# A selective scan on one core: the tiles that feed it, cut in half

## The chip, the cores and the metric

The kernel runs on one core of a Trainium2 chip. The core has four engines that compute: TensorE (PE, with its weight loads PEld), VectorE (DVE), ScalarE (ACT) and GpSimd (POOL). SyncE (SP) issues nearly all of this kernel's DMA transfers, one after the other in the order of its queue. The metric is device time in microseconds (us) of one execution.

## The reference, cut to what matters

Two layers on an image batch x of shape (4, 384, 32, 32). The first is a selective scan in four directions (rows, columns, and both backwards) with a normalization and GELU, followed by a mixture of four experts of which each token takes two. The second is attention and a small feed-forward layer. The change touches the scan alone:

```python
xs = _cross_scan(x)                               # 4 directions k, 1024 positions l
x_dbl = jnp.einsum('bkdl,kcd->bkcl', xs, x_proj_weight)
dts, Bs, Cs = (x_dbl[:, :, :R], x_dbl[:, :, R:R + N], x_dbl[:, :, R + N:])   # R = 12, N = 16
dts = jnp.einsum('bkrl,kdr->bkdl', dts, dt_projs_weight)
A = -jnp.exp(A_logs.astype(jnp.float32)).reshape(K, D, N)
dt = jax.nn.softplus(dts + dt_projs_bias[None, :, :, None])
...
def step(h, inp):
    dtt, ut, bt, ct = inp
    dA = jnp.exp(dtt[..., None] * A)
    h = h * dA + (dtt * ut)[..., None] * bt[:, :, None, :]
    y = jnp.einsum('bkdn,bkn->bkd', h, ct)
    return (h, y)
```

For each of 384 channels d and 16 states n there is one recurrence along the 1024 positions. It needs dt and dt * u of its channel, and B and C of its state.

## The kernel before, in words

**Stages.** `scan_layer` goes through 32 units: 4 images b, 4 directions k, 2 halves of 512 positions (`HF = 512`). After the last unit of an image, `finish` normalizes it, and `between` starts the tail of the image before: its experts (`experts`, eleven slots of 256 tokens), its attention and its last layers. A scheduler orders the instructions of each engine by its own timeline, so that the tail of image b - 1 stands between the instructions of the scan of image b. Only the tail of the last image comes after the scan. Each engine, SP too, works through its instructions in the order so fixed.

**Projection.** `project` (L287) makes a unit's inputs, one unit ahead. A matmul gives dt, B and C for 512 positions (`xd_ps`, L312), ACT copies it (`xd`), SP stores the B and C rows in DRAM (`rows`, L318), and loads them back into `bcs` tiles, each row spread over 32 partitions (L325). Then, in three parts of 128 channels, ACT, POOL (L360, L361) and DVE (L366, L367) make dt and dt * u, and SP stores both in DRAM (`dd`, L369 and L370).

**A tile's layout.** The 128 partitions of a scan instruction hold 32 channels times 4 states. So `bcs` has B and C of 4 states in 4 bands of 32 partitions, and the 16 states make 4 groups (`NG = 4`). `dtr` has 32 channels repeated for the 4 states, for two blocks of channels side by side (j = 0, 1). One `bcs` tile holds B and C (t) of two groups, 8 KB per partition; one `dtr` tile holds dt (s = 0) and dt * u (s = 1) of two blocks, 8 KB per partition. Both come from pools with three buffers. Each band and each t or s is a transfer of its own, 128 KB: 8 for a tile.

**The scan.** `chunk` (L373) does 128 channels of a unit; a unit has three chunks, the whole scan 96. It loads two `dtr` tiles (q = 0, 1; L386). Then, for each of the 4 groups and each q:
- POOL multiplies dt * u by B for both blocks (L401, 1024 elements per partition),
- ACT makes exp(dt * A) into `da` in PSUM, one instruction per block (L410); `da` has two buffers,
- DVE scans (L415), one instruction per block,
- for q = 1, DVE multiplies by C (L422); for q = 0, POOL does (L429),
- PE sums over the states into `acc` (L436), one instruction per block.

POOL thus has three instructions of 1024 elements per group, twelve per chunk. In its queue, L401 of a group usually stands some instructions ahead of L429 of the group before.

**When a buffer is free.** A `dtr` tile is last read in the fourth group of its chunk, by POOL's L401 (dt * u) and by ACT's second L410 (dt). A `bcs` tile is last read in the third chunk of its unit, by POOL's L429 and DVE's L422. The load of the next tile in that slot waits for these on SP's queue, and everything behind it on that queue waits with it: other `dtr` and `bcs` loads, the stores of `dd` and `rows`, and in the expert stage the weights (`w<-in_w`, 576 KB each, L757 and L765), which wait for PE to be done with their slot.

Of the kernel before, what the change touches and what calls it, by code (L numbers as in the profile page):

```python
# [9 lines left out]
F32 = mybir.dt.float32  # L10
I32 = mybir.dt.int32
AF = mybir.ActivationFunctionType
# [5 lines left out]
P = 128  # L18
# [5 lines left out]
HF = 512  # L24
# [20 lines left out]
DB = 32  # L45
NB = D // DB
NJ = P // DB
NG = NS // NJ
# [56 lines left out]
def halves(i):  # L105
    return slice(i * HF, (i + 1) * HF)


class Body:
# [76 lines left out]
    def scan_layer(self, x1, between):  # L186

        nc, tc, a = self.nc, self.tc, self.a
        with ExitStack() as ctx:
# [58 lines left out]
            for n, unit in enumerate(units):  # L248
# [3 lines left out]
                if n + 1 < len(units):  # L252
                    nb = units[n + 1][0]
                    if nb not in us:
                        us[nb] = start(nb)
                    project = self.project(units[n + 1], us[nb], wx, work, dram, psum, ahead)
                    next(project)
# [29 lines left out]
    def project(self, unit, u, wx, work, dram, psum, made):  # L287

        nc, a = self.nc, self.a
        b, k, i = unit
        by_cols = k % 2 == 1
        w = slice(i * (HW // NH), (i + 1) * (HW // NH))

        def part(c):
            if by_cols:
                return u[:, c, :].rearrange("p (h w) -> p w h", h=HW)[:, w, :]
            return u[:, c, halves(i)]  # L300

        def split(ap):
            return ap.rearrange("p (w h) -> p w h", h=HW) if by_cols else ap

        def k2(name, shape=(P, HF)):
            return work.tile([*shape], F32, tag="k2", name=name, bufs=6)

        wdt = k2("wdt", (R, D))
        nc.sync.dma_start(out=wdt, in_=a["wdt"][:, k, :])
        ps = psum.tile([P, HF], F32, tag="ps", name="xd_ps")  # L310
        for c in range(DC):
            nc.tensor.matmul(  # L312
                split(ps[:XD, :]), wx[:, c, k, :], part(c), start=(c == 0), stop=(c == DC - 1)
            )
        xd = k2("xd", (XD, HF))
        nc.scalar.copy(xd, ps[:XD, :])
        rows = dram.tile([2 * NS, HF], F32, tag="rows", name="rows")
        nc.sync.dma_start(out=rows, in_=xd[R:XD, :])  # L318
        view = rows.rearrange("(t g n) l -> n t g l", t=2, g=NG)
        bcs = []  # L320
        for h in range(NG // 2):
            bc = work.tile([P, 2, 2, HF], F32, tag="bcs", name="bcs", bufs=3)
            for n in range(NJ):
                for t in range(2):
                    nc.sync.dma_start(  # L325
                        out=bc[n * DB : (n + 1) * DB, t],
                        in_=view[n, t, 2 * h : 2 * h + 2].partition_broadcast(DB),
                    )
            bcs.append(bc)

        dd = dram.tile([2, D, HF], F32, tag="dd", name="dd")
        made += [bcs, dd]
        yield

        def begin(c):
            ps = psum.tile([P, HF], F32, tag="ps", name="dt_ps")
            nc.tensor.matmul(ps, wdt[:, c * P : (c + 1) * P], xd[:R, :], start=True, stop=True)  # L340
            bias = self.col("dtb", k * DC + c)
            mag, one_e, lnw = k2("mag"), k2("one_e"), k2("lnw")
            nc.scalar.activation(mag, ps, AF.Abs, bias=bias)
            nc.scalar.activation(ps, ps, AF.Relu, bias=bias)
            nc.scalar.activation(mag, mag, AF.Exp, scale=-1.0)
            nc.scalar.activation(one_e, mag, AF.Identity, bias=1.0)
            nc.scalar.activation(lnw, one_e, AF.Ln)
            nc.scalar.activation(one_e, one_e, AF.Identity, bias=self.minus1)  # L348
            return ps, mag, one_e, lnw

        def behind(engine):
            if self.place_behind is None:
                return nullcontext()
            return self.tc.issue_after(self.place_behind[engine])

        for c in range(DC):
            ps, mag, one_e, lnw = begin(c)
            yield
            with behind("pool"):
                nc.gpsimd.tensor_sub(mag, one_e, mag)  # L360
                nc.gpsimd.tensor_sub(lnw, lnw, mag)  # L361
            yield
            d, du = mag, one_e
            rows = slice(c * P, (c + 1) * P)
            with behind("dve"):
                nc.vector.tensor_add(ps, ps, lnw)  # L366
                nc.vector.tensor_mul(split(du), split(ps), part(c))  # L367
            nc.scalar.copy(d, ps)  # L368
            nc.sync.dma_start(out=dd[0, rows, :], in_=d)  # L369
            ins = nc.sync.dma_start(out=dd[1, rows, :], in_=du).ins  # L370
        made.append(ins)

    def chunk(self, unit, first, c, fed, carry, nega, sel, acc, work, dap):  # L373

        nc = self.nc
        b, k, i = unit
        bcs, dd, _ = fed
        dtr = []  # L380
        for q in range(NJ // 2):
            t = work.tile([P, 2, 2, HF], F32, tag="dtr", name="dtr", bufs=3)
            at = c * P + q * 2 * DB
            for n in range(NJ):
                for s in range(2):
                    nc.sync.dma_start(  # L386
                        out=t[n * DB : (n + 1) * DB, s],
                        in_=dd[s, at : at + 2 * DB, :].rearrange("(j d) l -> d j l", d=DB),
                    )
            dtr.append(t)  # L390

        def run(ap):
            return ap[:, ::-1] if k >= 2 else ap

        last = 0 if k >= 2 else HF - 1
        for g in range(NG):
            bc = bcs[g // 2]
            out = []
            for q in range(NJ // 2):
                bx = work.tile([P, 2, HF], F32, tag="bx", name="bx", bufs=6)  # L400
                pool = nc.gpsimd.tensor_mul(  # L401
                    bx, dtr[q][:, 1], bc[:, 0, g % 2].unsqueeze(1).to_broadcast([P, 2, HF])
                ).ins
                cg = bc[:, 1, g % 2]
                at = ((c * 2 + q) * NG + g) * 2
                for j in range(2):
                    block = c * NJ + 2 * q + j
                    col = (k * NB + block) * NG + g
                    da = dap.tile([P, HF], F32, tag="da", name="da")
                    nc.scalar.activation(  # L410
                        da, dtr[q][:, 0, j, :], AF.Exp, scale=nega[:, col : col + 1]
                    )
                    hold = carry[:, at + j : at + j + 1]
                    h = bx[:, j, :] if q == 0 else da
                    nc.vector.tensor_tensor_scan(  # L415
                        run(h), run(da), run(bx[:, j, :]), 0.0 if first else hold,
                        ALU.mult, ALU.add,
                    )
                    if q == 1:
                        if first:  # L420
                            nc.vector.tensor_copy(hold, h[:, last : last + 1])
                        dve = nc.vector.tensor_mul(bx[:, j, :], h, cg).ins  # L422
                if q == 0:
                    if first:
                        for j in range(2):
                            nc.vector.tensor_copy(
                                carry[:, at + j : at + j + 1], bx[:, j, last : last + 1]
                            )
                    pool = nc.gpsimd.tensor_mul(  # L429
                        bx, bx, cg.unsqueeze(1).to_broadcast([P, 2, HF])  # L430
                    ).ins
                out.append(bx)
            for q in range(NJ // 2):
                for j in range(2):
                    lo = (2 * q + j) * DB
                    nc.tensor.matmul(  # L436
                        acc[lo : lo + DB, :], sel, out[q][:, j, :],
                        start=(g == 0), stop=(g == NG - 1),
                    )
            self.place_behind = {"pool": pool, "dve": dve}  # L440
            yield
# [428 lines left out]
    def attention(self, xc, sums, room):  # L870
# [71 lines left out]

        steps = [(t, i, j) for t in range(HEADS // 2) for i in range(NH) for j in range(MB)]
        made = [project(0)]
        ahead = scores(0, made[0][0], 0, 0)
        atts = []
# [363 lines left out]
```

## Time and profile before

| | us |
|---|---|
| Median of 3 runs | 4761.76 (4757.81 to 4772.4) |
| The profiled execution, its own time | 4754.72 |
| its span, first to last instruction | 4751.4 |
| Scan, first to last L401 | 64.1 to 3644.8 |
| POOL busy in the span | 3098.0 |
| of it L401, 768 instructions of 2.376 us | 1802.4 |
| of it L429, 384 instructions of 2.376 us | 911.4 |
| DVE busy | 3005.0 |
| PE busy | 3543.9 |
| ACT busy | 2568.9 |

The median is of runs without the profiler's one execution; the profile explains the latter, so its stages add up to its span of 4751.4 us. "Busy" counts time in which an engine executes. A line such as `X L1 <- Y L2: 10.0, 3, 5.0` among the waits says that X sat idle for 10.0 us in total before its instruction of line 1, in 3 waits, the longest 5.0, each ended by Y's instruction of line 2 or, where it says DMA, by the landing of that transfer. On a time line a bracket shows the idle time just before an instruction and what ended it; runs of like instructions are merged (x11). The costs of SP's transfers stand as the time of their issue, not of their landing.

Where the scan's main engines stood in forty slices of the span (119 us each), tenths busy:

```profile
DVE  4888887778888776977786668896886210001101
...
POOL 5999997688898777778887679978886110001000
```

### The profile page before, as it was taken

The page shows a single profiled execution, that of the slowest core. Times are in us where ns is not written, and L with a number is a line of the kernel's source. Part 1 is how long each engine was busy: PE and PEld are TensorE (multiplying, and loading weights), DVE is VectorE, ACT ScalarE, POOL GpSimd, SP SyncE. Part 2 cuts the span into 40 slices and gives each one's busy share as a digit, 9 for nine tenths or more (in the row PEclk, how much of TensorE's full clock was granted, in tenths as well). Part 3 has the DMA queues.
Part 4 walks back from the last instruction along what each step waited for, and adds up shares of the span by engine and source line. Part 5 has one row for each costly group of instructions (what it writes and reads, how often), then busy time and mean ns, then how long its engine had stood idle before and what let it go on. Part 6 is the DMA issues. An engine that isn't in the chain of part 4 may idle for free.

```text
span 4751.4 us, 46823 instructions
## 1 busy us (share of the span) xinstructions
PE 3543.9 (75%) x13984; PEld 1707.0 (36%) x13984; DVE 3005.0 (63%) x4308; ACT 2568.9 (54%) x4406; POOL 3098.0 (65%) x1515
## 2 busy tenths in 40 slices
PE   4343334579997688757998767866999889998797
PEld 1000001235554222214555422233556655554323
DVE  4888887778888776977786668896886210001101
ACT  4445544446665666555565566756665344333454
POOL 5999997688898777778887679978886110001000
PEclk6555556579998788868999878977999999998797
DMA  4454463468877434446888444446795743342100
GB/s 108 107 125 106 108 165 85 125 206 222 233 213 210 127 93 113 122 137 181 223 225 240 130 138 106 112 123 181 209 253 169 252 159 127 105 132 77 43 16 14
DMA packets 412229, 691.86 MB, mean 146 GB/s; under 512 B 51136, under 2 KB 214336, under 8 KB 411968
## 3 DMA queue, kind: packets, MB, share of 16 engines
q1 hardware_dynamic: 403232, 663.24, 50.6%
q0 software_dynamic: 8192, 25.17, 1.6%
q8 instruction: 112, 1.84, 0.2%
q14 instruction: 149, 1.22, 0.1%
q10 hardware_dynamic: 544, 0.40, 0.0%
HBM read 563.83 MB, written 124.78 MB: 145 GB/s over the span
## 4 chain that ended last, share of the span: by engine, by line
PE 39%; DVE 20%; DMA 11%; POOL 10%; ACT 9%; issue 7%; SPq 3%; another core or an unknown queue 1%; DVEq 0%; POOLq 0%; ACTq 0%
PE h_ps L803 10%; PE y_ps L819 10%; DVE da L415 6%; POOL bx L401 6%; DMA dtr<-dd 6%; DVE bx L415 5%; PE s_ps L911 4%; PE o_acc L960 3%; PE acc L436 3%; POOL bx L429 2%; ACT da L410 2%; DVE bx L422 2%; PE xd_ps L312 2%; DMA bcs<-rows 2%; DMA w<-in_w 2%
## 5 line engine op out<-in xcount | busy, mean ns | idle before, releaser
L401 POOL TENSOR_TENSOR bx<-dtr,bcs 128x1024 f32<-128x1024 f32 x768 | 1802.4, 2376 | 298.4 <-DMA dtr<-dd 167.9
L410 ACT ACTIVATE da<-dtr,nega 128x512 f32<-128x512 f32 x1536 | 1043.7, 689 | 1107.3 <-DVE bx L422 662.4
L429 POOL TENSOR_TENSOR bx<-bx,bcs 128x1024 f32<-128x1024 f32 x384 | 911.4, 2376 | 128.1 <-DVE bx L415 48.4
L436 PE MATMUL acc<-bx,sel 128*32 128x512 f32 x3072 | 543.8, 751 | 536.7 <-POOL bx L429 401.7
L803 PE MATMUL h_ps<-xc,w 128*128 128x256 f32 x3168 | 780.1, 399 | 83.6 <-DVE xc L787 39.0
L819 PE MATMUL y_ps<-w,hs 128*128 128x384 f32 x2112 | 736.7, 501 | 27.0 <-ACT hs L812 21.4
L803 PEld LDWEIGHTS h_ps<-xc,w 128*128 128x128 f32 x3168 | 617.3, 199 | 302.7 <-issue 122.8
L415 DVE TENSOR_TENSOR_SCAN bx<-da,carry,bx 128x512 f32<-128x512 f32 x384 | 473.3, 1269 | 120.5 <-ACT da L410 61.8
L415 DVE TENSOR_TENSOR_SCAN bx<-da,bx 128x512 f32<-128x512 f32 x384 | 453.3, 1210 | 134.3 <-POOL bx L401 82.7
L415 DVE TENSOR_TENSOR_SCAN da<-da,carry,bx 128x512 f32<-128x512 f32 x384 | 477.1, 1274 | 93.3 <-POOL bx L401 56.8
L819 PEld LDWEIGHTS y_ps<-w,hs 128*128 128x128 f32 x2112 | 401.0, 194 | 359.1 <-issue 83.5
L415 DVE TENSOR_TENSOR_SCAN da<-da,bx 128x512 f32<-128x512 f32 x384 | 455.4, 1218 | 101.9 <-POOL bx L401 56.7
L422 DVE TENSOR_TENSOR bx<-da,bcs 128x512 f32<-128x512 f32 x768 | 508.9, 679 | 3.1
L1001 POOL TENSOR_TENSOR xt<-xt,wb 128x3072 f32<-128x3072 f32 x4 | 26.8, 6706 | 688.0 <-DMA wb<-in_wb 688.0
L916 ACT ACTIVATE ex<-s_ps 128x512 f32<-128x512 f32 x512 | 299.7, 591 | 251.8 <-PE s_ps L911 251.2
L436 PEld LDWEIGHTS acc<-bx,sel 128*32 128x32 f32 x3072 | 74.6, 119 | 875.5 <-POOL bx L429 556.6
L911 PE MATMUL s_ps<-w 64*128 64x512 f32 x1024 | 308.4, 679 | 89.0 <-ACT ex L916 88.6
L960 PE MATMUL o_acc<-ex,vt 128*64 128x512 f32 x1024 | 299.9, 664 | 0.7 <-ACT att L968 0.6
L808 ACT ACTIVATE hs<-h_ps,bb 128x256 f32<-128x256 f32 x528 | 211.5, 472 | 159.3 <-PE h_ps L803 152.2
L823 DVE TENSOR_TENSOR y<-y_ps,bb 128x384 f32<-128x384 f32 x88 | 48.3, 549 | 361.0 <-PE y_ps L819 345.5
L360 POOL TENSOR_TENSOR mag<-one_e,mag 128x512 f32<-128x512 f32 x96 | 123.2, 1283 | 96.8 <-ACT one_e L348 96.6
L340 PE MATMUL dt_ps<-xd,wdt 12*128 12x512 f32 x192 | 138.8, 811 | 60.6 <-ACT mag L368 34.9
(189 smaller groups left out, 3777.4 us busy)
## 6 DMA issues: line engine op xcount, KB each, us to landing
w<-in_w SPq DMA_DIRECT2D x352, 576.0 KB
dtr<-dd SPq DMA_DIRECT2D x1536, 128.0 KB
bcs<-rows SPq DMA_DIRECT2D x512, 128.0 KB
dd<-one_e SPq DMA_DIRECT2D x96, 256.0 KB
dd<-mag SPq DMA_DIRECT2D x96, 256.0 KB
rows<-zero SPq DMA_DIRECT2D x88, 192.0 KB
xs<-rows SPq DMA_DIRECT2D x44, 384.0 KB
made<-y SPq DMA_DIRECT2D x44, 384.0 KB
```

What stands on the lines that cost most here:

```text
L401: pool = nc.gpsimd.tensor_mul(bx, dtr[q][:, 1], bc[:, 0, g % 2].unsqueeze(1).to_broadcast([P, 2, HF])).ins
L410: nc.scalar.activation(da, dtr[q][:, 0, j, :], AF.Exp, scale=nega[:, col : col + 1])
L415: nc.vector.tensor_tensor_scan(run(h), run(da), run(bx[:, j, :]), 0.0 if first else hold, ALU.mult, ALU.add,)
L422: dve = nc.vector.tensor_mul(bx[:, j, :], h, cg).ins
L429: pool = nc.gpsimd.tensor_mul(bx, bx, cg.unsqueeze(1).to_broadcast([P, 2, HF])).ins
L436: nc.tensor.matmul(acc[lo : lo + DB, :], sel, out[q][:, j, :], start=(g == 0), stop=(g == NG - 1),)
L803: nc.tensor.matmul(ps[:, r, :], w1[(f + r) // wf][:, c, (f + r) % wf * P : ((f + r) % wf + 1) * P], xc[:, c, :], start=(c == 0), stop=(c = ...
L808: nc.scalar.activation(hs[:, f + r, :], ps[:, r, :], AF.Identity, bias=bb[:, f + r : f + r + 1])
L819: nc.tensor.matmul(out[:, :D], hs[:, f, t * P : (t + 1) * P], w2[f // wf][:, f % wf, :], start=(f == 0), stop=(f == FC - 1),)
L911: nc.tensor.matmul(ps[:, o, :], w[rows, j * P : (j + 1) * P], w[rows, halves(i)], start=True, stop=True,)
L916: ins = nc.scalar.activation(ex[:, o, :], ps[:, o, :], AF.Exp, scale=HD**-0.5, accum_out=sums[:, t, 2 * j + o, i : i + 1],).ins
L960: ins = nc.tensor.matmul(out[cols, :], made[t][1][:, j, cols], ex[:, o, :], start=(j == 0), stop=(j == MB - 1),).ins
```

## The change

The two kinds of input tile are cut in half. A `dtr` tile holds dt or dt * u, not both, and there are seven of 4 KB for three of 8 KB (28 KB for 24 KB per partition). A `bcs` tile holds B and C of one group, not of two, and there are five of 4 KB for three of 8 KB (20 KB for 24 KB). The transfers stay as many, and each moves 128 KB as before; those of `bcs` take B and C of one group in place of B or C of two. The order in which the loads are written changes with it: for `dtr`, all four bands of dt come ahead of those of dt * u. Lines behind the change shift by one.

```diff
-        for h in range(NG // 2):
-            bc = work.tile([P, 2, 2, HF], F32, tag="bcs", name="bcs", bufs=3)
+        for g in range(NG):
+            bc = work.tile([P, 2, HF], F32, tag="bcs", name="bcs", bufs=5)
             for n in range(NJ):
-                for t in range(2):
-                    nc.sync.dma_start(
-                        out=bc[n * DB : (n + 1) * DB, t],
-                        in_=view[n, t, 2 * h : 2 * h + 2].partition_broadcast(DB),
-                    )
+                nc.sync.dma_start(
+                    out=bc[n * DB : (n + 1) * DB], in_=view[n, :, g].partition_broadcast(DB)
+                )
             bcs.append(bc)
...
         for q in range(NJ // 2):
-            t = work.tile([P, 2, 2, HF], F32, tag="dtr", name="dtr", bufs=3)
+
+            pair = []
             at = c * P + q * 2 * DB
-            for n in range(NJ):
-                for s in range(2):
+            for s in range(2):
+                t = work.tile([P, 2, HF], F32, tag="dtr", name="dtr", bufs=7)
+                for n in range(NJ):
                     nc.sync.dma_start(
-                        out=t[n * DB : (n + 1) * DB, s],
+                        out=t[n * DB : (n + 1) * DB],
                         in_=dd[s, at : at + 2 * DB, :].rearrange("(j d) l -> d j l", d=DB),
                     )
-            dtr.append(t)
+                pair.append(t)
+            dtr.append(pair)
...
-            bc = bcs[g // 2]
+            bc = bcs[g]
...
-                    bx, dtr[q][:, 1], bc[:, 0, g % 2].unsqueeze(1).to_broadcast([P, 2, HF])
+                    bx, dtr[q][1], bc[:, 0].unsqueeze(1).to_broadcast([P, 2, HF])
                 ).ins
-                cg = bc[:, 1, g % 2]
+                cg = bc[:, 1]
...
-                        da, dtr[q][:, 0, j, :], AF.Exp, scale=nega[:, col : col + 1]
+                        da, dtr[q][0][:, j, :], AF.Exp, scale=nega[:, col : col + 1]
```

## The prediction

> **What bounds the kernel now.** I read the busy times by stage first, then who waits in the stages, then single boundaries on the time line. The stages are eight stretches of the span; each row gives PE, PEld, DVE, ACT and POOL busy time with instruction counts, then the granted clock, the DMA share and GB/s.
>
> ```profile
> 64.00:600.00 536.00, 199.43 (x628) 29.07 (x632) 468.03 (x621) 265.80 (x418) 534.42 (x249) 0.53 0.46 111
> ...
> 1000.00:1500.00 500.00, 462.93 (x1868) 274.52 (x1869) 409.47 (x525) 323.57 (x503) 440.25 (x205) 0.95 0.78 215
> 1500.00:2130.00 630.00, 444.46 (x1736) 151.95 (x1734) 479.67 (x707) 374.02 (x701) 470.87 (x235) 0.79 0.46 124
> 2130.00:2650.00 520.00, 452.50 (x1860) 273.95 (x1861) 385.31 (x521) 312.70 (x478) 411.78 (x190) 0.93 0.75 207
> ```
>
> Up to 600 us only the scan runs, and POOL is busy 534 of 536 us: it is the bound, and no earlier load can help there. From 600 to 3660 us the tail of the batch before runs in between, and nothing is full: in the expert stages (1000 to 1500, 2130 to 2650, 3260 to 3660) PE is at 463/500, 453/520 and 357/400, POOL at 80 to 88%. Only there can a stall be worth anything. Who waits for the tiles that the change cuts, over the whole span:
>
> ```profile
> POOL bx L401 <- DMA dtr<-dd: 167.9, 48, 10.5
> ...
> ACT da L410 <- DMA dtr<-dd: 124.5, 43, 9.7
> ```
>
> Walking POOL's time line, 47 of the 48 waits stand at one place: the second half (q = 1) of the first group of a chunk. A wait of ordinary length, POOL first, then SP:
>
> ```profile
> 2888.43 2.35 POOL L429 TENSOR_TENSOR bx<-bx,bcs 128x1024 f32<-128x1024 f32 x1
> 2893.70 2.36 POOL L401 TENSOR_TENSOR bx<-dtr,bcs 128x1024 f32<-128x1024 f32 x1 [2.92 <-DMA dtr<-dd]
> ```
>
> ```profile
> 2885.97 6.08 SPq L386 DMA_DIRECT2D dtr<-dd  x11
> ```
>
> The reason is the rotation of three tiles. A chunk uses two (q = 0, 1), the third holds the next chunk's q = 0; the next q = 1 needs the slot of this chunk's q = 0. That is free once POOL has read its dt * u and ACT its dt for the last time, in the last group; here ACT's da ended at 2885.90 and SP went at 2885.97. Eight transfers must then be issued and land, while POOL has some 8 us of other work left. A second boundary, where eight bcs loads stand ahead of the late tile:
>
> ```profile
> 1519.61 3.24 SPq L325 DMA_DIRECT2D bcs<-rows  x7
> 1522.95 8.81 SPq L386 DMA_DIRECT2D dtr<-dd  x16
> ```
>
> The slot was free at 1517.9, the loads began at 1522.95, and POOL idled 5.99 us. Sixteen issues took 8.81 us here; in the quiet part (361.82 us) they took 7.35, so one issue is 0.46 to 0.55 us.
>
> **The change part by part.** The count and size of transfers stay: 1536 for dtr and 512 for bcs, 128 KB each, with the same runs of 2 KB. No POOL, ACT or DVE instruction changes its shape. So removed and added work is nothing; only when a slot is free and what waits in SP's queue differ.
>
> *dtr, seven tiles of 4 KB.* A chunk takes four (dt and dt * u of q = 0 and 1). Three more hold the next q = 0 and its q = 1 dt, so only dt * u of q = 1 is late: four transfers for eight, and ACT's wait for the late dt goes. In the built order of the changed kernel, this tile waits for one engine, POOL or ACT, not for both. I price only the issue: from the 4th to the 8th transfer of each waiting boundary in the trace is 1.9 us in quiet places and 2 to 8 us where weights stream. I sorted the 47 waits by chunk of the unit (three per unit) and took from each the smaller of its length and that stretch:
> - third chunk: 13 waits, 31.0 us, of which 25.7 goes.
> - second chunk: 18 waits, 65.7 us; 42.7 goes. Here the next unit's bcs stand ahead, eight loads now, none or four after; up to four issues of 0.46 us more make it 54.9.
> - first chunk: 16 waits, 68.6 us; 52.5 would go if nothing stood ahead.
>
> *bcs, five tiles.* A unit uses four, and one is ahead: the next unit's group 0. Groups 1, 2 and 3 need groups 0, 1 and 2 of the old unit to be done (DVE's last L422, POOL's L429, of its third chunk). Before, groups 2 and 3 went together when group 1 was done, some 14 us (two groups of 3 x 2.36 us on POOL) ahead of the boundary. Now the group 3 load waits for group 2, done just as the boundary comes. In the built SP order it stands directly ahead of the late dtr tile at 13 of the 31 unit starts, with its four issues (1.9 us), and behind it in the queue stand that tile, the further dtr tiles, and in the expert stages weight loads. Its own use, in group 3 of the first chunk, is 20 us off, so bcs itself need not be late. At those 13 starts the four issues saved are given back, and the wait on DVE's L422 comes no later than the release that is waited for today, since ACT's last da of q = 0 waits for the same L422:
>
> ```profile
> ACT da L410 <- DVE bx L422: 662.4, 359, 12.7
> ```
>
> So I take nothing there (their waits were 41 of the 68.6 us) and 22 us at the other starts. POOL's waits fall by 26 + 55 + 22 = 103 us, of 168. Both ends for the step: 133 if the 13 starts gain too; 64 if each loses 3 us (four issues plus a late L422).
>
> *How much of it reaches the end.* Of the 171 us that the stretches list (a wait across a border counts twice), 97 lie in the expert stages (26.7, 55.6, 14.6) and 71 in the others after 600 us (12.1, 32.8, 26.5). In the expert stages PE has only 37 + 67 + 43 = 147 us of idle time left, and much of what POOL no longer waits will turn into waits for PE or DVE: I take half. Elsewhere PE is at 44 to 73% and DVE at 76 to 79%: I take three quarters. With 103/168 = 0.61: 0.61 x 97 x 0.5 + 0.61 x 71 x 0.75 = 30 + 32 = 62 us. The bounds are 0 and the whole, and past it: if chains after the wait (DVE's 254 us of waits for L401) shorten too, 150.
>
> *Order.* The scheduler moved little: on POOL at most 3 instructions, on PE 40 more tail matmuls stand ahead of the scan's last one. After 3660 us PE is busy 975.54 us with 3960 records, 0.25 us each, and a built matmul is two records (1536 for acc are 3072 in the trace): 40 are 20 us that the end may lose. Bounds 0 and 20 us; I take 10.
>
> Sum: 62 + 10 = 72 us. The profiled execution took 4754.72 us (span 4751.4 and 3.3 around it), so 4683; the median, 4761.76, is 7 us above it, so the forecast is 4690 us.
>
> A rule against the change stands in the Trainium skill, "DMA: Bandwidth & Descriptors", section Bandwidth: batch transfers to 1 MiB or more. By that page's fit for GpSimd-issued transfers, 2.0 us and bytes over 436 GB/s, a late tile of 1 MB counted as one transfer would take an estimated 4.4 us and one of 512 KB 3.2 us, so that halving saves 1.2 us a boundary; on 47 boundaries at the shares above that would be some 35 us in all for the 62. The rows decide: transfers stay at 128 KB here, and the eight issues alone take 3.7 us, so the stretch falls with their count.
>
> **The rivals.**
> 1. *The idle time only moves.* POOL's next bx comes sooner, but then PE's acc, DVE's L422 or ACT's da is awaited, all of which already alternate in the waits. For it: PE at 93% in one expert stage, batch 0 where the chain shows dtr at 8.7% and POOL never idles. Against: 71 us of the waits lie where no engine is above 83%. Realised 0 to 15%: 4750 to 4770; 4760.
> 2. *More goes than I count.* Some slots are freed by POOL alone, 2 to 7 us ahead of ACT, and the w loads queued behind dtr go earlier as well. Then nearly all 168 us go and two thirds or more of it comes off, with the order's 10: about 120 us; 4640.
> 3. *SP's queue blocks at unit starts (slower).* The group 3 load, or the next unit's rows<-xd store, which at some starts stands ahead of the last dtr tile, is not ready; everything behind it waits, dtr and weights alike. SP's rows<-xd waits today are 128.9 us in 19, up to 23.4 us, so the raw material is there. A loss of 6 us at 25 starts after 600 us is 150 us on POOL; at the shares above (0.6) it is 90, less a gain of 60 at the other boundaries: 4792. It decides once a start loses over 4 us on average.
>
> **How the numbers follow.** About 0.3%, 14 us, is what a measurement of this kernel tells from no change. Chances: the forecast (gain of 30 to 100 us) 0.47, rival 2 0.19, rival 1 0.12, rival 3 0.22. Faster is the forecast, rival 2 and a sliver of rival 1: 0.67; same 0.11; slower 0.22. The likeliest case alone gives 4660 to 4735. The range for 8 in 10 reaches from 4615 (rival 2 with 147 us) to 4790 (rival 3 at its price).
>
> **What would show it.** POOL L401 waits for dtr should fall from 168 to 40 to 100 us, those that stay at first chunks of units; ACT's 124.5 us for dtr to under 50. The first 600 us should not move. SP's waits at the bcs line, 185 us for DVE L422 now, should grow in number, not in harm: POOL waits for bcs, 9.2 us now, should stay under 20. If SP shows long waits at bcs or rows<-xd right ahead of dtr, rival 3 holds; if POOL's dtr waits fall and its others grow by as much, rival 1.

## The result, and the profile after

The changed kernel takes 4766.77 us (median of 20 runs, 4754.09 to 4778.67) against 4756.07 us for the kernel before on the same chip: a ratio of 1.0025 with a 95% interval of 1.0013 to 1.0036. The forecast was 4690 us. So there is no gain but a small loss, some 11 us. The profiled execution of after took 4754.09 us (span 4752.3), that of before 4754.72 (span 4751.4). The former is the shortest of after's 20, 13 us under their median, so the two profiles don't show the loss.

The wait that the change was priced by is nearly gone. First the list of who waited for whom, GpSimd's part, in before and then in after; the columns are the total in us, the number of waits and the longest.

```profile
POOL bx L401 <- PE acc L436: 112.3, 18, 37.2
...
POOL bx L429 <- DVE bx L415: 48.4, 22, 8.0
POOL bx L429 <- DVE carry L426: 29.9, 17, 4.2
```

```profile
POOL bx L402 <- PE acc L437: 139.2, 34, 46.5
...
POOL bx L430 <- DVE bx L416: 90.0, 43, 7.7
POOL bx L430 <- DVE carry L427: 72.4, 31, 6.5
POOL bx L402 <- DMA dtr<-dd: 26.7, 14, 4.8
...
POOL bx L430 <- DMA bcs<-rows: 2.2, 2, 1.6
```

The waits for `dtr` fell from 167.9 us to 26.7, those for `bcs` stayed small. But three other rows grew: TensorE's return of a `bx` tile from 112.3 to 139.2, the scan's result (`bx`) from 48.4 to 90.0, the carry (the last value of a scan, kept for the next) from 29.9 to 72.4, together by 111 us. The rows of GpSimd's two kinds of work, before and then after, show the exchange in the idle time before them, behind the second bar:

```profile
L401 POOL TENSOR_TENSOR bx<-dtr,bcs 128x1024 f32<-128x1024 f32 x768 | 1802.4, 2376 | 298.4 <-DMA dtr<-dd 167.9
...
L429 POOL TENSOR_TENSOR bx<-bx,bcs 128x1024 f32<-128x1024 f32 x384 | 911.4, 2376 | 128.1 <-DVE bx L415 48.4
```

```profile
L402 POOL TENSOR_TENSOR bx<-dtr,bcs 128x1024 f32<-128x1024 f32 x768 | 1794.7, 2365 | 180.7 <-PE acc L437 139.2
...
L430 POOL TENSOR_TENSOR bx<-bx,bcs 128x1024 f32<-128x1024 f32 x384 | 903.9, 2361 | 221.1 <-DVE bx L416 90.0
```

118 us went from the first and 93 came to the second. ScalarE's list shows the same, 124.5 us for the late `dt` before and now

```profile
ACT da L411 <- DMA dtr<-dd: 38.1, 25, 3.0
```

while its waits for VectorE inside the scan rose from 924 to 1002 us.

VectorE is where much of the time went. Its waits for GpSimd's `bx` ahead of a scan of `da` fell from 114 to 21 us. Yet in the seven stretches from 64 to 3660 us it was busy 2848 us before and 2898 after, in 3956 and 3961 instructions: 50 us that it no longer idled came back as longer instructions. TensorE's last `acc` matmul of the scan ended at 3652.0 us before and at 3640.1 after. The table by stages, in the same columns as before the change:

```profile
64.00:600.00 536.00, 196.90 (x634) 30.70 (x633) 465.54 (x621) 265.40 (x414) 532.84 (x249) 0.57 0.41 113
...
1500.00:2130.00 630.00, 436.72 (x1748) 155.88 (x1748) 498.27 (x702) 377.71 (x700) 470.98 (x235) 0.78 0.41 121
...
2650.00:3260.00 610.00, 416.28 (x1668) 134.05 (x1668) 511.97 (x694) 382.90 (x711) 503.25 (x249) 0.78 0.43 123
```

In 1500 to 2130 us VectorE is busy 498 us with 702 instructions, where it was 480 with 707. What grew is shown by the time line of VectorE and GpSimd around one addition of 128 x 16 elements (columns: start, time taken, engine, line, operation):

```profile
2867.50 6.98 POOL L402 TENSOR_TENSOR bx<-dtr,bcs 128x1024 f32<-128x1024 f32 x3
...
2872.27 10.35 DVE L925 TENSOR_TENSOR inv<-sums 128x16 f32<-128x16 f32 x1
2874.43 1.28 POOL L359 TENSOR_TENSOR lnw<-lnw,mag 128x512 f32<-128x512 f32 x1
2875.64 2.35 POOL L430 TENSOR_TENSOR bx<-bx,bcs 128x1024 f32<-128x1024 f32 x1
2877.94 4.65 POOL L402 TENSOR_TENSOR bx<-dtr,bcs 128x1024 f32<-128x1024 f32 x2
2882.55 0.68 DVE L423 TENSOR_TENSOR bx<-da,bcs 128x512 f32<-128x512 f32 x1
...
2883.26 0.69 ACT L411 ACTIVATE da<-dtr,nega 128x512 f32<-128x512 f32 x1 [11.50 <-DVE bx L423]
```

The addition has a median of 0.176 us, and here it took 10.35. It ended at 2882.62, 0.03 us after GpSimd's last instruction of an unbroken run (2877.94 + 4.65 = 2882.59), ScalarE idled 11.50 us behind it, and GpSimd itself then stood 4.59 us for VectorE's `bx`, until 2887.18. I call such an instruction *held*. Its inputs are the two columns of `sums`, both in SBUF. Of after's sixteen additions, the seven that began while GpSimd worked took 1.63 to 10.35 us, the nine others 0.18 at most; in before it is seven with 0.23 to 12.75 and nine with 0.18 at most. The long ones, over 6 us, are five in after and two in before, and each ended 0.03 us after an unbroken run of GpSimd.

The normalisations of `xt` (L513 and L631, 128 x 384) are held too, mostly for one GpSimd instruction at a time: 0.47 us undisturbed, and in after 16 of the 40 in the scan took 1.41 to 7.43, all but one of them at most 2.56. Each of the 16 ended 0.22 us after the end of a GpSimd instruction, and for 11 of them GpSimd went straight on with the next. Summed over VectorE's instructions in the scan, the time above the shortest of the same kind (excesses over 0.3 us, whatever their reason) is 96 us before and 149 after; `inv` has 27 and 47 of it, the normalisations 8 and 33.

After the scan nothing was won either: from its last matmul to the end 1099.4 us before, 1112.2 after. The experts of the third image do end sooner (3767 us for 3799), but then TensorE stands idle at the hand-over to the last image:

```profile
3803.14 0.20 DVE L508 RECIPROCAL rstd<-rstd 128x8 f32<-128x8 f32 x1 [1.58 <-issue]
...
3820.66 0.39 SPq L850 DMA_DIRECT2D x<-xt  x1
3821.37 1.67 SPq L776 DMA_DIRECT2D xs<-rows  x2
3827.32 3.20 DVE L513 TENSOR_SCALAR xt<-xt,mv,rstd 128x384 f32<-128x384 f32 x8 [23.97 <-DMA x<-xt]
3827.85 0.18 PEld L864 LDWEIGHTS tc_ps<-ident,xt 128*128 128x128 f32 x1 [56.37 <-DVE xt L513]
```

The normalisation overwrites `xt` and waits for the store of the same tile to DRAM (L850). `xt` was ready at 3801, and SP issued the store at 3820.66; in its queue nine loads of expert numbers into registers (L749) stand ahead of it, from 3798.5 to 3820.

### The profile page after: what moved, and what is told of

Same layout as the page of the kernel before. It is cut to its first block, busy times and chain, and to the rows that moved or that the text cites. A ratio compares the mean times of both kernels' runs of the same rounds, so it can differ in the third digit from the quotient of the medians.

```text
span 4752.3 us, 47256 instructions
## 1 busy us (share of the span) xinstructions
PE 3508.4 (74%) x13984; PEld 1700.4 (36%) x13984; DVE 3054.3 (64%) x4308; ACT 2573.4 (54%) x4406; POOL 3097.6 (65%) x1515
## 4 chain that ended last, share of the span: by engine, by line
PE 37%; DVE 25%; POOL 11%; issue 9%; ACT 9%; DMA 6%; SPq 2%; another core or an unknown queue 0%; DVEq 0%; POOLq 0%; ACTq 0%
PE y_ps L820 10%; PE h_ps L804 9%; DVE da L416 8%; DVE bx L416 7%; POOL bx L402 6%; PE s_ps L912 3%; POOL bx L430 3%; PE o_acc L961 3%; PE acc L437 3%; DVE bx L423 3%; ACT da L411 3%; DMA dtr<-dd 3%; PE xd_ps L312 2%; PE o_ps L1008 1%; PE w_ps L889 1%
## 5 line engine op out<-in xcount | busy, mean ns | idle before, releaser
L402 POOL TENSOR_TENSOR bx<-dtr,bcs 128x1024 f32<-128x1024 f32 x768 | 1794.7, 2365 | 180.7 <-PE acc L437 139.2
L437 PE MATMUL acc<-bx,sel 128*32 128x512 f32 x3072 | 558.4, 755 | 507.2 <-POOL bx L430 426.5
L804 PE MATMUL h_ps<-xc,w 128*128 128x256 f32 x3168 | 761.7, 393 | 49.0 <-DVE xc L788 29.8
```

Of the source, the lines that this page charges most:

```text
L402: pool = nc.gpsimd.tensor_mul(bx, dtr[q][1], bc[:, 0].unsqueeze(1).to_broadcast([P, 2, HF])).ins
L437: nc.tensor.matmul(acc[lo : lo + DB, :], sel, out[q][:, j, :], start=(g == 0), stop=(g == NG - 1),)
L804: nc.tensor.matmul(ps[:, r, :], w1[(f + r) // wf][:, c, (f + r) % wf * P : ((f + r) % wf + 1) * P], xc[:, c, :], start=(c == 0), stop=(c = ...
```

## The experiments

A kernel's profile is one execution. Two kernels with all but the same order (e2 and f2 below) ended their scans 19 us apart in their profiles, so single ends of the scan are read to some 20 us only, and verdicts rest on the ratios to the kernel before, with their intervals.

**e1: the order at the hand-over.** In after, the sixteen gathers of the third image stand ahead of the sixteen scatters of the last one in GpSimd's queue, in before behind them. The edit orders the scatters first (the planner then moved some tail work in the other queues as well):

```diff
                 body.route(B - 1, x1, wide)
+                for got in gathers:
+                    for put in body.slots[1]:
+                        tc.add_manual_dep(
+                            got, put.name,
+                            mybir.DependencyInfo(mybir.DependencyClass.NoSync, mybir.DependencyReason.DATA),
+                            reason="order",
+                        )
```

> The changed kernel with one order fixed: on POOL the sixteen scatters of the last image's tokens (rows<-xt) stand ahead of the sixteen gathers of the image before (got<-made), as they do in the kernel before; the scheduler had swapped them. Theory (the gain of the loads is lost at the hand-over from scan to tail, where PE idles 56 us at 3772 to 3828): that hole shrinks to about 20 us and the time falls by 20 to 35 us from 4767, to 4730 to 4747, under the kernel before. Rival (the swap is not on the path, the scan gave nothing): 4760 to 4770.

Measured: 4777.46 us, ratio 1.0045 (1.0030 to 1.0060), not below after's 1.0025 and above both forecasts. TensorE still idles there for 43 us, from 3762 to 3805. Undoing the swap of gathers and scatters won nothing; my theory of the hand-over fell.

**e2: the held addition.** The sum of the two columns as a reduction, which has one input; every queue keeps its order, instruction for instruction.

```diff
-            nc.vector.tensor_add(inv, sums[:, t, :, 0], sums[:, t, :, 1])
+            nc.vector.tensor_reduce(inv, sums[:, t], AX.X, ALU.add)
```

> The changed kernel with the eight additions inv<-sums done as a reduction over one input, nothing else moved in any queue. Theory (a DVE addition of two SBUF inputs does not run while POOL works without a break, and POOL has fewer breaks now): the seven of them in the scan, 46.8 us over their 0.17 us in the changed kernel and 27.3 us in the kernel before, fall under 0.5 us each, DVE's busy time falls by about 45 us, and the scan ends 15 to 40 us earlier; the time falls by 0 to 35 us, less if the hand-over eats it. Rival (the long additions are a wait for something else, such as the sums): they stay long, time unchanged at 4760 to 4772.

Measured: 4741.63 us, ratio 0.9962 (0.9948 to 0.9975), 0.6% below after. One tiny instruction, sixteen times in the kernel, was worth 25 to 30 us (by the medians and by the ratios). The list of the operations on `inv` (least, median and longest duration in ns) in e2, in after and in before:

```profile
L925 DVE TENSOR_REDUCE inv<-sums x16: 158/186/189, 1649.4 to 4625.1; 128x16 f32<-128x32 f32 x16
```

```profile
L925 DVE TENSOR_TENSOR inv<-sums x16: 175/176/10354, 1648.6 to 4653.3; 128x16 f32<-128x16 f32 x16
```

```profile
L924 DVE TENSOR_TENSOR inv<-sums x16: 164/176/12754, 1689.8 to 4651.3; 128x16 f32<-128x16 f32 x16
```

No reduction is held, though seven of them began while GpSimd worked, and the scan ends at 3614.3 us. A part of the holding moved on: another product of VectorE (`wc`, L995), 0.55 us undisturbed, now took 10.38 and 6.27 us where after has 1.26 at most, and all excesses together fell from 149 to 112 us only. The Trainium skill, "SBUF — State Buffer", section "Who interferes with whom", says that a VectorE instruction with two inputs in SBUF contends with a GpSimd instruction that reads SBUF, and that a reduction never does on this chip. The runs agree. The page (section "SBUF: two separate sides") also has the one that starts first keep the shared pair of ports for the whole instruction while the other blocks; by that the addition would wait for the rest of one GpSimd instruction, at most 2.4 us by the rows here, where the time line above shows the rest of one and four more going first.

**e3 and e4: the two halves of the change alone.** e3 has `bcs` in five tiles of one group beside the old `dtr`; e4 has `dtr` in six tiles of 4 KB beside the old `bcs` (seven do not fit beside it).

```diff
+        for g in range(NG):
+            bc = work.tile([P, 2, HF], F32, tag="bcs", name="bcs", bufs=5)
...
+                t = work.tile([P, 2, HF], F32, tag="dtr", name="dtr", bufs=6)
```

> The kernel before with B and C alone in five tiles of one group, dt and dt * u as before. Theory (the bcs part costs and gains nothing): POOL's waits for dtr stay at 140 to 180 us, bcs waits under 20 us, time within 15 us of the kernel before. Rival (the group 3 loads ahead of the late dtr tile block SP's queue): POOL's waits for dtr grow past 200 us and the time is 20 to 60 us above the kernel before.

> The kernel before with dt and dt * u in six tiles of 4 KB for three of 8 KB, B and C as before (seven do not fit beside them): the same room, freed in smaller pieces. Theory (the depth of the seventh tile and the halved late load do the work): dt and dt * u of q = 1 are both late, eight transfers as before, and POOL's waits for dtr fall only to 90 to 150 us; time within 20 us of the kernel before. Rival (the finer release alone does it): POOL's waits for dtr fall under 60 us, as in the changed kernel.

Measured: e3 4786.12 us, ratio 1.0053 (1.0039 to 1.0067); e4 4760.93 us, ratio 1.0008 (0.9991 to 1.0024). In e4 GpSimd's waits for `dtr` are 56.1 us, as the rival said: the finer tiles alone take two thirds of them, and still no time is won. In e3 they are 123.7 us, under both forecasts, while the time is 25 us longer. Its waits for `bcs` look dear at first:

```profile
POOL bx L399 <- DMA bcs<-rows: 40.7, 1, 40.7
POOL bx L427 <- DMA bcs<-rows: 8.9, 2, 5.4
```

But the 40.7 us are one wait at 1689 us, where an image ends; before has 28.6 us at that place, after 30.8, put down to TensorE's `acc`. Without it some 9 us remain. That e3 is 0.5% slower is measured; by what, these lines don't tell, and its queues have another order too.

**f1, f2, f3, f4: what the released time meets next.** f1 is the kernel before with e2's reduction (from the second image's experts on the planner then orders it differently). f2 is e2 with the store of the hand-over issued by ScalarE:

```diff
-        nc.sync.dma_start(out=self.tokens(b), in_=xt)
+        nc.scalar.dma_start(out=self.tokens(b), in_=xt)
         return xt
```

f3 is e2 with one buffer moved from `dtr` to `bx`, and f4 is e4 with the reduction.

```diff
-                t = work.tile([P, 2, HF], F32, tag="dtr", name="dtr", bufs=7)
+                t = work.tile([P, 2, HF], F32, tag="dtr", name="dtr", bufs=6)
...
-                bx = work.tile([P, 2, HF], F32, tag="bx", name="bx", bufs=6)
+                bx = work.tile([P, 2, HF], F32, tag="bx", name="bx", bufs=7)
```

> The kernel before, with the sum of two columns in divide (inv) made by a reduction with one input in place of an addition of two; the planner's order differs from before's from the second image's experts on. My theory, that this instruction is held while GpSimd's instructions follow each other without a break: before has 27 us of such holding against 47 in the changed kernel, so the scan ends 8 to 20 us sooner than 3652 and the time is 4738 to 4750; then the change, with that instruction out of the way (4741.6), is worth 0 to 10 us. Rival, that the reduction gains by itself whatever GpSimd does: 20 to 26 us as in the changed kernel, 4731 to 4737, and the change is a loss of 5 to 10 us even then.

> The changed kernel with the one-input reduction, and the combine's store of xt to DRAM issued by ScalarE in place of SyncE. My theory of TensorE's idle stretch of 55 us at the hand-over to the last image (3745 to 3800): the normalisation there overwrites xt and waits for the store, which SyncE issues some 19 us after xt is ready, because nine loads of expert numbers into registers and their follow-ups stand ahead of it. Then the store lands near 3782, the normalisation stands some 15 to 20 us sooner, and the time falls by 10 to 20 us to 4722 to 4732. Rival: the stretch is set by the scatters of the last image's rows, so the transposes come sooner but TensorE idles after them as long, and the time stays within 4 us of 4741.6.

> The changed kernel with the one-input reduction, six dtr tiles and seven bx tiles (the same room); the planner's order differs all through. Theory A: GpSimd's remaining idle time at L402 (133 us for TensorE's return of a bx tile) is what holds the scan; a seventh tile takes 50 us or more of it, the scan ends 15 to 35 us sooner than 3614 and the time is 4705 to 4730. Theory B, as in the result of the change itself: the waits move to the next edge (the carry, DVE's own products, dtr); GpSimd's idle total in the scan stays within 30 us and the time within 10 us of 4741.6.

> The kernel before with dtr in six 4 KB tiles, B and C as they were, and the one-input reduction: the change's gain without its second half. My theory, that B and C in five tiles cost 20 us or more by themselves and that the held instruction hides the gain: time 4725 to 4742, not above the changed kernel with the same reduction (4741.6). Rival, that the seventh tile pays for the shorter ring of B and C: 4745 to 4755.

Measured, as ratios to before: f1 1.0036 (1.0020 to 1.0052), f2 0.9947 (0.9930 to 0.9964), f3 1.0094 (1.0076 to 1.0111), f4 0.9968 (0.9951 to 0.9985).

f1 missed both forecasts: the reduction made the kernel before slower. Its scan ended where before's did (3651.3 us for 3652.0) though 27 us of holding were gone, and the rest took 1120.3 us for 1099.4. So here clearing the held additions gave the scan nothing that one profile can show, and the loss lies after it; as the order changed in both, f1 does not say what the additions cost in before's own order. f4 met my forecast, 0.4% under e4: its order is nearly e4's, the same on GpSimd and SP, so it bears out e2, where no order changed.

f2's lines at the hand-over:

```profile
3791.54 0.37 ACTq L850 DMA_DIRECT2D x<-xt  x1
...
3803.09 3.21 DVE L513 TENSOR_SCALAR xt<-xt,mv,rstd 128x384 f32<-128x384 f32 x8 [9.33 <-issue]
```

The store leaves as soon as `xt` is done, though it then needs 11.5 us to the normalisation, where SP's took 6.7 in after. TensorE's idle stretch shrank from 55 to 41 us. The time fell by 0.15% against e2, with intervals that overlap: the mechanism is seen, and its worth, some 8 us for the 10 to 20 that I forecast, isn't proven.

f3 fits neither forecast in time; of the two theories it bears out B, that the waits move, with a loss on top. With a seventh `bx` tile GpSimd's waits for TensorE hardly fell (133.1 us in e2), those for the carry doubled (72.7), and those for `dtr`, which gave up a tile, went from 19.8 to 56.8:

```profile
POOL bx L430 <- DVE carry L427: 145.4, 47, 9.2
POOL bx L402 <- PE acc L437: 127.6, 19, 45.0
```

GpSimd's idle time moved to other edges again, and here, with a new order all through, the kernel took 1.3% more than e2.

**g1 and g2: the second held instruction.** g1 is f2 with the normalisations made by ScalarE; g2 is f4 with the store by ScalarE.

```diff
-            self.nc.vector.tensor_scalar(
-                out[:, m, :], xt[:, m, :], mean[:, m : m + 1], rstd[:, m : m + 1],
-                op0=ALU.subtract, op1=ALU.mult,
-            )
+            self.nc.scalar.activation(
+                out[:, m, :], xt[:, m, :], AF.Identity, bias=bias[:, m : m + 1], scale=rstd[:, m : m + 1]
+            )
...
+        nc.scalar.activation(bias, mean, AF.Copy, scale=-1.0)
+        for m in range(MB):
+            nc.scalar.activation(
+                bias[:, m : m + 1], bias[:, m : m + 1], AF.Copy, scale=rstd[:, m : m + 1]
+            )
```

> f2 (changed kernel, one-input reduction, store by ScalarE) with the two normalisations (xt from xt, mean, rstd; 40 instructions of 0.47 us in the scan) made by ScalarE from a bias that ScalarE works out too; the planner's order differs from the first image's routing on. My theory, that VectorE's held instructions cost time in the dense order: 33 us of holding and some 16 us of work leave VectorE, ScalarE gains some 30 us where it has room, and the time falls by 8 to 25 us from 4733 to 4708 to 4725. Rival, as the seventh bx tile showed: the next edge takes the time and the new order decides, 4733 to 4760.

> f4 (the kernel before with dtr in six 4 KB tiles and the one-input reduction) with the combine's store issued by ScalarE; order otherwise as f4. Theory, that the store's issue behind SyncE's register loads costs each hand-over some microseconds whatever the tiles of B and C: 8 us less than f4, 4728 to 4738, equal to f2 (4733), so that the second half of the change brings nothing. Rival: f4's order at the hand-over has the store off the path, time within 3 us of 4741.

Measured: g1 4703.01 us, ratio 0.9889 (0.9864 to 0.9914), 0.6% below f2; g2 4750.20 us, 0.9989 (0.9974 to 1.0003). g1 went the way that I forecast, by 27 to 30 us for 8 to 25, and is faster than before and after, by 1.1% and 1.4%. g2 met neither forecast: no gain over f4.

**h1 and h2: the change itself, with nothing held by these two.** h1 is the kernel before with g1's three edits, h2 is e4 with them.

> The kernel before with the same three edits as g1 (one-input reduction, store by ScalarE, normalisations by ScalarE), so that g1 against this is the change itself with the held instructions out of the way. My theory, that the change's finer release is worth something once VectorE's instructions no longer need GpSimd's gaps: before's 171 us of dtr waits stay, the holding that is removed was small there (27 and 8 us), so 4735 to 4760 against g1's 4703, and the change is then worth 30 to 55 us. Rival, that g1's gain is ScalarE's taking of work and a good order, whatever the tiles: 4700 to 4715.

> dtr in six 4 KB tiles, B and C as before, and g1's three edits. Theory: the finer release alone carries the change's worth, and B and C in single groups only pay for the seventh tile: 4700 to 4720, within 10 us of g1. Rival, that the seventh tile is what makes g1 fast: 4725 to 4750, nearer to h1.

Measured: h1 4746.08 us, ratio 0.9976 (0.9961 to 0.9991); h2 4709.37 us (of four runs), 0.9888 (0.9863 to 0.9912). Both forecasts of my theory held. GpSimd's waits in h1, and then in g1:

```profile
POOL bx L401 <- PE acc L436: 158.9, 26, 41.0
POOL bx L401 <- DMA dtr<-dd: 141.2, 42, 10.4
...
POOL bx L429 <- DVE bx L415: 61.8, 25, 11.8
POOL bx L429 <- DVE carry L426: 50.4, 22, 6.6
```

```profile
POOL bx L430 <- DVE bx L416: 96.1, 40, 6.5
POOL bx L402 <- PE acc L437: 94.4, 30, 25.2
...
POOL bx L430 <- DVE carry L427: 63.8, 29, 7.0
POOL bx L402 <- DMA bcs<-rows: 28.6, 1, 28.6
...
POOL bx L402 <- DMA dtr<-dd: 21.4, 8, 4.9
```

The waits for `dtr` fall by 120 us, and this time the other rows take back little: those for TensorE fall by 64, less the one wait of 28.6 us, which is a pause at an image's end as in e3 (there are two such pauses, 41.0 and 41.0 us in h1, 25.2 and 28.6 in g1, so most of this fall is theirs); `bx` and the carry rise by 48. GpSimd's idle time in the scan is 567 us in h1 and 506 in g1. VectorE's excesses are alike in the cleared kernels, 83 us in h1, 88 in g1 and 87 in h2: here the change adds no holding. TensorE's last `acc` matmul starts at 3657.8 us in h1 and at 3593.0 in g1.

All ratios to the kernel before, side by side (rows: edits made beside the tiles; columns: how the tiles are cut):

| | `dtr` 3 x 8 KB, old `bcs` | `dtr` 6 x 4 KB, old `bcs` | the change |
|---|---|---|---|
| nothing else | 1 | 1.0008 | 1.0025 |
| reduction (f1, f4, e2) | 1.0036 | 0.9968 | 0.9962 |
| and store by ScalarE (g2, f2) | | 0.9989 | 0.9947 |
| and normalisation by ScalarE (h1, h2, g1) | 0.9976 | 0.9888 | 0.9889 |

Read along the last row, the change is worth 0.9889 / 0.9976 = 0.991, some 41 us (0.988 to 0.994 from both intervals, as the root of the sum of their squares). Read along the second it is 0.993, some 35 us, of which f1's longer tail (1120.3 us for e2's 1111.2) makes 9. Read along the first it is worth nothing. In the middle column the six smaller `dtr` tiles do as well as the whole change in the second and the last row; in the third they lag by 0.4%. That the seventh tile, and with it the halved `bcs` that makes room for it, adds anything is not shown.

## Why the prediction was wrong

**What bounds the kernel** was read rightly in part: to 600 us nothing moved (GpSimd busy 532.84 of 536 us, 534.42 before). That nothing is full after that was true of busy shares, and it was the wrong ground to count on.

**Waits of GpSimd**: forecast a fall of 103 us, with 133 as the upper end; measured 141 (167.9 to 26.7). ScalarE's waits for `dt` fell to 38.1 as asked. The rotation, the four issues for eight and the release by one engine are thus right and were priced low. That the remaining waits would stand at first chunks of units held for 6 of the 13 that stand at the second half of a chunk's first group.

**bcs, "I take nothing there"**: in the changed kernel that stands. Its waits fell to 2.2 us, and SP's own waits at that line went from 20 with 184.8 us to 34 with 137.9, more and shorter. But e3, with that half alone, is 0.5% slower, which the working had no term for. Rival 3, the queue blocked at unit starts, is not seen.

**"How much of it reaches the end"** is the step that failed. It took 62 us, by a half and three quarters of each stage's waits; 12 us came at the scan's end, which is within what one profile can tell from none. The step read idle time on TensorE and GpSimd as room. It didn't ask which instructions of other engines lived in GpSimd's pauses: the long holds of VectorE's addition ended at such a pause, two in before and five in after. GpSimd's idle time in the scan is 564 us before and 552 after, while VectorE's excesses rose by 53. e2 shows that the held additions alone cost after 25 to 30 us, with nothing else changed. In g1 against h1, where the change adds no holding, it gains 41 us, two thirds of the 62 that the step had promised; the orders of these two differ.

That the missing waits are what lengthened the holds is likely, not shown. In the four kernels with no other edit, waits for `dtr` and excesses go against each other (168 and 96 us in before, 124 and 114 in e3, 56 and 131 in e4, 27 and 149 in after), but each of the four has its own order, and that too decides which of VectorE's instructions meet a busy GpSimd. Rival 1, that the idle time only moves, which had a chance of 0.12, is what happened, and its reason was in none of its sentences: it named TensorE's `acc`, VectorE's L422 and ScalarE's `da` as the next to wait for, not instructions that grow.

**Order**: 10 us were taken for 40 tail matmuls that go ahead of the scan's end. They did: the third image's experts ended 32 us sooner. The gain was lost at the next wait, the hand-over, where TensorE's idle time after the scan rose from 110 to 145 us. The bounds of 0 to 20 left out a loss; the rest after the scan grew by 13 us.

**The rule set against the change**, batching transfers, gave an estimated 35 us for the 62; the 41 us of the cleared kernels lie between the two, and no run here separates them.

**What stays open.** The planner orders queues anew with most edits (h1 and g1 differ in order, e2 and after do not), and kernels with a new order can differ by as much: f1 and f3, edited to be faster, lost 0.4% against before and 1.3% against e2. So the 41 us hold for these orders; that h2, with an order of its own, gained as much as g1 speaks against luck and doesn't rule it out. Why e3 and f1 are slower was not settled, nor why g2 didn't gain.

## What to carry to other kernels

Before counting a stall that goes as time won, look at what other engines do in that pause: list the instructions whose longest duration is far above their least, and see whether they end when the busy engine stops. A pause that another engine needs isn't idle time to be won, and an engine's stalls are priced together with its neighbours' longest instructions. Clear the held instructions first (here a reduction for an addition, and ScalarE for a normalisation); in the orders built here, the finer tiles then paid.

## What the runs showed of the hardware

An addition of 128 x 16 elements with both inputs in SBUF took up to 12.75 us in before and 10.35 in after, for 0.176 us undisturbed. These two outlasted the rest of one GpSimd instruction and four or five more that followed without a pause, and ended 0.03 us after the last of them; two short holds in after (1.63 and 1.91 us) ended between two GpSimd instructions. The same sum as a reduction took 158 to 189 ns in all sixteen places, seven of them begun while GpSimd worked. The normalisations, with one SBUF tensor and two per-partition operands, were held as well, 33 us in all in after, but mostly for one GpSimd instruction at a time (15 of 16 took 1.41 to 2.56 us). Made by ScalarE they took 690 to 707 ns in every one of the 64 instances.
